# Two graph-attention layers on one core: mask steps placed earlier in the interleaving, softmax sums of two head groups in one PSUM bank, value differences per batch

## Chip, cores and metric

The kernel runs on one core of one Trainium2 chip. The metric is the device time of an execution in microseconds; lower is better. The runs of the kernel before have a median of 2573.73 us (2572.56 to 2574.11, three runs).

## What is computed

64 graphs (the batch) of 256 nodes with 512 features each pass through two attention layers over one adjacency matrix; all data is fp32. In both, the input is normalised over its features and cut at zero, and the layer's output is added to the input:

```
h = max(layernorm(x), 0)
x = x + concat(softmax(mask(leaky_relu(s_i + n_j))) @ (h W), h W)      # layer 0, one head of 256
h = max(layernorm(x), 0)
q, k, v = h Wq' + bq, h Wk' + bk, h Wv' + bv                           # layer 1, 8 heads of 64
x = x + softmax(mask(q k' / 8)) @ v @ Wo' + bo
```

## The kernel before

**Tiling and stages.** The 64 graphs are handled in 32 groups of two ("batches" b = 0 and 1 of group g). A group passes through five stages, and in the steady part four groups are under way at once:

- `first_norm` (layer 0's normalisation of group g+3): statistics on DVE, the factors (a power and a product on POOL), the scaled and cut rows `xn` on ACT, a transposition by DVE and by a pass through DRAM (`passed`, `moved`, issued by SP), and the copy into `hT0` on ACT.
- `first_layer` (group g+2): products `ph`, copied to `H` by ACT, a broadcast transposition `pn` of a column of `H` for the neighbour scores, exponentials `e`, products `po`, and layer 1's normalisation, which ends in `hT1`. Its last piece, the 14th, calls `operand_sums(gpsimd, ...)`: four POOL operations of 128x512 that make `sums` and change a quarter of `hT1` (lines 473 to 479, 613 to 614). There is one `sums` buffer (line 596).
- `project` (group g+1): q, k and v by a scheme with seven block products instead of eight (lines 634 to 708); its third, fifth and seventh products read `sums`, and the very last, for v, ends the project stage of a group. ACT keeps partial results in tiles with the tag `kept`; DVE adds them.
- `scores` (group g, batch b): eight score tiles `sc` on PE and their exponentials into `p` on ACT, then four mask pieces (`mask_pairs`, line 738): DVE multiplies a pair of heads by the 0/1 mask, POOL adds the second key half to the first, in place.
- `weigh` (line 752) and `outputs` (line 785) of the batch whose scores came last: the sums of the exponentials over the keys (`total`, a product with ones), their reciprocal `r` on DVE, the weighted values `pr`, their scaling into `oT`, and the output products `py`, which DVE adds onto `x`.

With P0 and P1 the two key halves of the exponentials, `p` holds P0 + P1 in the place of P0 after the mask pieces. So `total` needs one product instead of two, and `v` must hold V0 and V1 - V0: (P0 + P1) V0 + P1 (V1 - V0) is the wanted sum. `value_differences` (line 710) makes V1 - V0 in place on POOL, for both batches of a group. In `pr` the four heads of a quad ("quad" is half of the eight heads) lie in the four column strips of PE; the products with V0 come first, then those with V1 - V0.

**What sets the order.** A scheduler orders each engine's instructions. The kernel ties it down: PE's instructions are chained one behind another as they are written (`in_order`, line 131), and `not_sooner` (line 123) puts an instruction behind the last one that was *written* for the same engine, which each engine's wrapper `Remembers` keeps in `last` (line 27). Instructions without such a tie may be moved by the scheduler. Engines then execute in that order.

What is written when is given by two strings, one for each batch of a group (line 882). A letter calls the next piece of one stage: `S` scores, `m` a mask piece, `n` first_norm, `s` first_layer, `u` project, `o` outputs. At half of each string (position 16 or 18, line 908) come the residual's bias additions for group g+1 (`residual`, four POOL operations), then the value differences of group g, both only in the first string, and the load of a later group. `weigh` comes ahead of each string, for the batch before. In the second string the 14th `s` stands at position 25 and an `n` that makes factors at position 23; in the first string the factors are made by the `n` at position 21.

**Buffers.** `q`, `k` and `v` of a group and batch lie in "places", single buffers of 4 KB per partition, taken from a list and given back when their reader is written (lines 625 to 629, 735, 779). PSUM has five banks in turn (`mm`, line 109) and three held ones. `r` has one buffer (line 764).

Of the kernel before, what the change touches and what calls it, by code (L numbers as in the profile page):

```python
# [8 lines left out]
F32 = mybir.dt.float32  # L9
# [5 lines left out]
P = 128  # L15
# [42 lines left out]
def bounded(  # L58
# [107 lines left out]

    w0_sb = const.tile([P, HP, F1 + 2], F32, name="w0_sb")
    nc.sync.dma_start(w0_sb[:, :, 2:], w0.rearrange("(c p) o -> p c o", p=P))
    adj_i = att.tile([P, NT, N], I32, tag="kept", name="adj_i")
    nc.sync.dma_start(adj_i, adj.rearrange("(t p) k -> p t k", p=P))  # L170

    def score_columns():
# [6 lines left out]
                )  # L179

    def mask():
        edge = att.tile([P, NT, N], F32, tag="kept", name="edge")
        not_sooner(vector, "tensor_scalar", edge, adj_i, 0.0, None, op0=ALU.not_equal)
        yield
        pt = mm("pt_mask").rearrange("p (k q) -> p k q", k=NT)
        for kb in range(NT):
            for t in range(NT):
                transpose(
                    pt[:, kb, t * P : (t + 1) * P], edge[:, t, kb * P : (kb + 1) * P], ident
                )  # L190
        not_sooner(vector, "tensor_copy", maskT, pt)

        not_sooner(vector, "reduce_max", bad[:, 0, :], edge, axis=AX.X)
        vector.tensor_scalar(bad[:, 0, :], bad[:, 0, :], 0.0, None, op0=ALU.is_equal)
        vector.tensor_tensor(edge, edge, adj_i, op=ALU.not_equal)
        vector.reduce_max(bad[:, 1, :], edge, axis=AX.X)
        yield
# [63 lines left out]
    def last_bias():  # L261


        wide = att.tile([P, 2, 2, P], F32, tag="kept", name="bv_wide")
        for q in range(NQ):
            for half in range(2):
                gpsimd.tensor_scalar(
                    wide[:, half, q, :], square_ones, bv_col[:, half, q : q + 1], None, op0=ALU.mult
                )
        yield  # L270
        pb = mm("pb")
        for q in range(NQ):
            for half in range(2):
                matmul(
                    pb, wide[:, half, q, :], w_sb["o"][:, half, 2 * q : 2 * q + 2, :],
                    start=(q == 0 and half == 0), stop=(q == NQ - 1 and half == 1),
                )
        yield
        not_sooner(vector, "tensor_add", b_out, pb, b_out)
        yield  # L280
# [341 lines left out]
                not_sooner(gpsimd, "tensor_add", xt, xt, b_out)  # L622


    places = [f"place{i}" for i in range(8)]

    def place(shape, name):
        tag = places.pop(0)
# [5 lines left out]
    def project(g):  # L634
        ops = operands.pop(g)
        for name in ("q", "k", "v"):
            shape = [P, NT, D] if name == "v" else [P, HP, N]
            dst = {}
            for b in range(GB):
                dst[b], tag = place(shape, f"{name}_{g}_{b}")  # L640
                qkv[name, g, b] = dst[b], tag
            turn[0] = 1 - turn[0]

            def blocks(bank):
                return bank.rearrange("p (o n) -> p o n", o=2)

            def product(out, i, start):
                a, w = ops[i][0], w_sb[name][:, :, ops[i][1], :]
                for o in range(2):
                    cols = slice(o * P, (o + 1) * P)  # L650
                    for c in range(2):
                        of, by = (a[:, c, cols], w[:, c, :]) if name == "v" else (w[:, c, cols], a[:, c, :])
                        matmul(
                            out[:, o, :], of, by, start=start and o == c == 0, stop=o == c == 1,
                            skip_group_check=True,
                        )

            def part(b, half):
                if name == "v":
                    return dst[b][:, :, half * D // 2 : (half + 1) * D // 2]  # L660
                return dst[b][:, 2 * half : 2 * half + 2, :]

            def take(to, bank, half):

                behind = [scalar.last] if g <= 1 else []
                if name == "v":
                    taken = [scalar.copy(to, bank)]
                else:
                    taken = [
                        scalar.activation(  # L670
                            to[:, o, :], bank[:, o, :], AF.Identity,
                            bias=bcol[name][:, 2 * half + o : 2 * half + o + 1], scale=1.0,
                        )
                        for o in range(2)
                    ]
                for last in behind:
                    for instruction in taken:
                        after(instruction, last)

            def kept(bank, half, i):  # L680
                s = att.tile([P, 2, N], F32, tag="kept", name=f"kept{i}_{name}_{g}")
                take(s, bank, half)
                return s

            first = blocks(held_bank(turn[0], f"p{name}1_{g}"))
            product(first, 1, True)
            p1 = kept(first, 0, 0)
            yield
            second = blocks(mm(f"p{name}2_{g}"))
            product(second, 2, True)  # L690
            vector.tensor_add(part(0, 0), second, p1)
            yield
            product(first, 6, False)
            p16 = kept(first, 0, 1)
            yield
            second = blocks(held_bank(1 - turn[0], f"p{name}7_{g}"))
            product(second, 7, True)
            p7 = kept(second, 1, 2)
            yield
            product(first, 5, False)  # L700
            vector.tensor_add(part(1, 1), first, p7)
            yield
            product(second, 4, False)
            vector.tensor_add(part(1, 0), second, p16)
            yield
            product(first, 3, False)
            take(part(0, 1), first, 1)
            yield

    def value_differences(g):  # L710

        for b in range(GB):
            v = qkv["v", g, b][0]
            not_sooner(gpsimd, "tensor_sub", v[:, 1, :], v[:, 1, :], v[:, 0, :])

    def scores(g, b):

# [34 lines left out]
    def weigh(g, b, p):  # L752


        v, v_tag = qkv["v", g, b]
        for quad in range(NQ):
            name = f"{g}_{b}_{quad}"
            total = mm(f"total_{name}")[:, :N]
            for j in range(QH):
                matmul(  # L760
                    total[j * S : (j + 1) * S, :], ones, p[:, quad * QH + j, 0, :],
                    start=True, stop=True,
                )
            r = att.tile([P, N], F32, tag="r", name=f"r_{name}", bufs=1)
            vector.reciprocal(r, total)
            pr = mm(f"pr_{name}").rearrange("p (h n) -> p h n", h=2)
            for half in range(2):
                for kb in range(NT):
                    for j in range(QH):
                        head = quad * QH + j  # L770
                        c0 = head * DH + half * S
                        matmul(
                            pr[j * S : (j + 1) * S, half, :], v[:, kb, c0 : c0 + S],
                            p[:, head, kb, :], start=(kb == 0), stop=(kb == NT - 1),
                        )
            oT = big.tile([P, 2, N], F32, tag=f"oT{quad}", name=f"oT_{name}", bufs=1)
            vector.tensor_mul(oT, pr, r[:, None, :].to_broadcast([P, 2, N]))
            oTs[quad] = oT
        places.append(v_tag)
        quads = [oTs[c][:, :, r * P : (r + 1) * P] for r in range(2) for c in range(2)]  # L780
        sums = big.tile([P, 3, 2, P], F32, tag="o_sums", name=f"o_sums_{g}_{b}", bufs=1)
        operand_sums(vector, quads, sums)
        operands["o", g, b] = seven(quads, sums)
# [95 lines left out]
    run(verdict)  # L879


    steps = ("Smmnuuuuonuouuomssnumnosunosnouso", "Smmsususuososuomssusumonusonuouunous")
    waiting, late = None, iter(())
    for g in range(NG):
        products = project(g + 1) if g + 1 < NG else iter(())
        pieces = first_layer(g + 2) if g + 2 < NG else iter(())
        for b, parts in enumerate(steps):
            if g == b == 0:

                parts = "Smmnn" + parts[4:].replace("uon", "unon", 1)  # L890
            if waiting is not None:
                weigh(*waiting)
                late = outputs(*waiting[:2])
            for i, part in enumerate(parts):
# [10 lines left out]
                else:  # L905
                    waiting = (g, b, scores(g, b))
                    masks = mask_pairs(waiting[2])
                if i == len(parts) // 2:
                    if b == 0:
                        if g + 1 < NG:  # L910
                            residual(g + 1)
                        value_differences(g)
                    if g + 3 < NG:
                        load(g + 3, b)
        run(products)
# [374 lines left out]
```

## Time and profile before

| | |
|---|---|
| median of three runs | 2573.73 us |
| the profiled execution's own time | 2571.85 us |
| its span, first to last instruction | 2570.2 us |
| mean granted TensorE clock | 0.998 |
| instructions | 41394 |
| value differences on POOL, 128x512 | 64, mean 1267 ns |
| reciprocals on DVE, 128x256 | 128, mean 1756 ns |
| mask multiplications on DVE, 128x1024 | 256, mean 1209 ns |
| mask sums on POOL, 128x512 | 256, mean 1603 ns |
| operand sums on POOL, 128x512 | 4 x 32, mean 1283 to 1289 ns |

The span and the waits are those of one profiled execution; its own time is 1.88 us below the median of the runs. PE's matmuls overlap: one of 256 columns is recorded with about 380 ns, and eight in a row begin 1.73 us apart from the next eight. PEld is the loading of weights. A matmul of fp32 leaves two records. In the steady part the timeline repeats itself once per group, so one group between two `sc` blocks can stand for nearly all.

### The profile page before, as it was taken

Reading aid. Unit: us, or ns where it says so; the run is one execution under the profiler, and the core shown is the slowest. Engines: PE = TensorE matmul, PEld = TensorE weight load, DVE = VectorE, ACT = ScalarE, POOL = GpSimd, SP = SyncE. Lnnn points to the kernel's source line nnn. Section 1 sums busy time; section 2 is a strip of 40 time slices with the busy share of each in tenths; the row PEclk is TensorE's granted clock in tenths of the full one; section 3 lists DMA queues with packets and bytes.
Section 4 is the critical chain, followed back from the end, with each engine's and each line's share of the span. In section 5 each row is a group of like instructions: output and inputs, shape, how many; then the busy total and the mean of one; then the engine's idle time right before and its main releaser. Section 6 shows DMA issues by size and latency. Waiting matters only on the chain.

```text
span 2570.2 us, 41394 instructions
## 1 busy us (share of the span) xinstructions
PE 2490.8 (97%) x16158; PEld 2052.6 (80%) x16158; DVE 1691.7 (66%) x2971; ACT 1012.5 (39%) x2019; POOL 1008.7 (39%) x978
## 2 busy tenths in 40 slices
PE   8999999999999999999999999999999999999998
PEld 7777878878778778788787887887887878878886
DVE  6566666776666666667766666666677666766656
ACT  5433443443433434434434344344344343443421
POOL 3524444243443334442444433344424444333432
PEclk9999999999999999999999999999999999999999
DMA  5122222322232321223222223212232222232110
GB/s 184 66 83 72 66 85 74 99 81 75 68 99 75 99 72 62 89 74 99 75 80 68 91 83 99 72 60 91 74 99 73 80 71 91 83 99 69 41 41 34
DMA packets 129353, 205.40 MB, mean 80 GB/s; under 512 B 13952, under 2 KB 78208, under 8 KB 129152
## 3 DMA queue, kind: packets, MB, share of 16 engines
q1 hardware_dynamic: 129152, 202.69, 24.7%
q8 instruction: 129, 2.11, 0.3%
q14 instruction: 72, 0.59, 0.1%
HBM read 104.08 MB, written 98.57 MB: 79 GB/s over the span
## 4 chain that ended last, share of the span: by engine, by line
PE 77%; POOL 14%; DVE 3%; issue 3%; ACT 2%; DMA 1%; POOLq 0%; SPq 0%; DVEq 0%; ACTq 0%
PE pq L137 15%; PE pv L137 15%; PE py L137 12%; PE sc L137 10%; PE pk L137 9%; PE pr L137 8%; POOL x L35 6%; PE po L137 4%; POOL p L35 4%; POOL v L35 3%; PE total L137 2%; DVE p L35 2%; ACT xn L35 1%; POOL factor L35 1%; PE ph L137 1%
## 5 line engine op out<-in xcount | busy, mean ns | idle before, releaser
L35 POOL TENSOR_TENSOR p<-p 128x512 f32<-128x512 f32 x256 | 407.8, 1603 | 970.9 <-DVE p L35 881.0
L35 ACT ACTIVATE p<-sc 128x512 f32<-128x512 f32 x512 | 264.0, 612 | 211.2 <-PE sc L137 203.3
L35 ACT ACTIVATE xn<-x,factor 128x512 f32<-128x512 f32 x256 | 194.4, 806 | 387.1 <-POOL factor L35 387.1
L35 DVE TENSOR_TENSOR x<-py,x 128x256 f32<-128x256 f32 x448 | 186.4, 416 | 243.8 <-PE py L137 234.6
L35 DVE TENSOR_TENSOR p<-p,maskT 128x1024 f32<-128x1024 f32 x256 | 301.5, 1209 | 0.0
L137 PE MATMUL sc<-q,k 64*128 64x256 f32 x2048 | 266.5, 390 | 8.0 <-ACT p L35 8.0
L35 DVE RECIPROCAL r<-total 128x256 f32<-128x256 f32 x128 | 224.8, 1756 | 66.3 <-PE total L137 59.9
L137 PE MATMUL py<-wo_sb,oT 128*128 128x256 f32 x1024 | 262.8, 379 | 3.5 <-DVE x L35 3.1
L137 PEld LDWEIGHTS sc<-q,k 64*128 64x128 f32 x2048 | 213.0, 186 | 62.1 <-issue 25.9
L35 DVE STREAM_TRANSPOSE xt<-xn 128x512 f32<-128x512 f32 x248 | 164.4, 692 | 134.2 <-ACT xn L35 134.2
L137 PE MATMUL pr<-p,v 128*32 128x256 f32 x4096 | 245.5, 379 | 0.4 <-POOL v L35 0.4
L137 PE MATMUL pk<-hT,wk_sb 128*128 128x256 f32 x1024 | 244.9, 382 | 0.0
L137 PE MATMUL pv<-wv_sb,hT 128*128 128x256 f32 x1024 | 238.6, 381 | 4.9 <-ACT kept_v L35 4.9
L137 PE MATMUL pq<-hT,wq_sb 128*128 128x256 f32 x1024 | 239.9, 382 | 0.0
L137 PE MATMUL ph<-w_sb,hT 128*128 128x258 f32 x1024 | 239.4, 381 | 0.3 <-ACT hT L35 0.3
L137 PEld LDWEIGHTS pv<-wv_sb,hT 128*128 128x128 f32 x1024 | 195.3, 191 | 32.2 <-ACT kept_v L35 5.3
L137 PEld LDWEIGHTS pk<-hT,wk_sb 128*128 128x128 f32 x1024 | 191.7, 190 | 36.1 <-issue 10.7
L137 PEld LDWEIGHTS pq<-hT,wq_sb 128*128 128x128 f32 x1024 | 191.8, 190 | 35.0 <-issue 9.9
L137 PEld LDWEIGHTS py<-wo_sb,oT 128*128 128x128 f32 x1024 | 193.8, 190 | 32.3 <-DVE x L35 3.9
L137 PEld LDWEIGHTS ph<-w_sb,hT 128*128 128x128 f32 x1024 | 194.4, 190 | 29.6 <-ACT hT L35 0.9
L137 PEld LDWEIGHTS pr<-p,v 128*32 128x32 f32 x4096 | 133.3, 110 | 88.6 <-POOL v L35 0.9
L35 POOL TENSOR_TENSOR factor<-factor,rexp 128x2 f32<-128x2 f32 x128 | 91.7, 716 | 281.2 <-DVE factor L35 281.2
(122 smaller groups left out, 3747.6 us busy)
## 6 DMA issues: line engine op xcount, KB each, us to landing
passed<-xt SPq DMA_DIRECT2D x124, 512.0 KB, 3.0
moved<-passed SPq DMA_DIRECT2D x496, 128.0 KB, 3.2
x<-in_x_dram SPq DMA_DIRECT2D x64, 512.0 KB, 4.3
out_dram<-x SPq DMA_DIRECT2D x64, 512.0 KB, 3.1
wq_sb<-in_L_gnn_Wq_dram SPq DMA_DIRECT2D x2, 512.0 KB, 9.2
wk_sb<-in_L_gnn_Wk_dram SPq DMA_DIRECT2D x2, 512.0 KB, 10.7
wv_sb<-in_L_gnn_Wv_dram SPq DMA_DIRECT2D x2, 512.0 KB, 7.5
wo_sb<-in_L_gnn_Wo_dram SPq DMA_DIRECT2D x8, 128.0 KB, 3.9
```

The costliest lines, as they stand in the source:

```text
L35: instruction = getattr(self.engine, operation)(*args, **kwargs)
L137: in_order(nc.tensor.matmul(*args, **kwargs))
```

## The change

Four things change:

- The third and fourth mask pieces of each batch are written earlier: in the first string at positions 8 and 11 instead of 15 and 20, in the second at 13 and 16 instead of 15 and 21. The other letters keep their order among themselves.
- `weigh` makes `total` of both quads in the two halves of one bank, then both reciprocals (now tied with `not_sooner`) in one tile `r`, then `pr` and `oT` of each quad.
- The value differences are made for one batch at a time, in each string at three quarters of its length (position 24 or 27) instead of both at half of the first.
- There are seven places instead of eight, each taken only when its part is first written, and three `kept` buffers instead of two.

```diff
-    places = [f"place{i}" for i in range(8)]
+    places = [f"place{i}" for i in range(7)]
...
-            dst = {}
-            for b in range(GB):
-                dst[b], tag = place(shape, f"{name}_{g}_{b}")
-                qkv[name, g, b] = dst[b], tag
...
             def part(b, half):
+                if (name, g, b) not in qkv:
+                    qkv[name, g, b] = place(shape, f"{name}_{g}_{b}")
+                to = qkv[name, g, b][0]
...
-                s = att.tile([P, 2, N], F32, tag="kept", name=f"kept{i}_{name}_{g}")
+                s = att.tile([P, 2, N], F32, tag="kept", name=f"kept{i}_{name}_{g}", bufs=3)
...
-    def value_differences(g):
-
-        for b in range(GB):
-            v = qkv["v", g, b][0]
-            not_sooner(gpsimd, "tensor_sub", v[:, 1, :], v[:, 1, :], v[:, 0, :])
+    def value_differences(g, b):
+
+        v = qkv["v", g, b][0]
+        not_sooner(gpsimd, "tensor_sub", v[:, 1, :], v[:, 1, :], v[:, 0, :])
...
+        name = f"{g}_{b}"
+        total = mm(f"total_{name}").rearrange("p (q n) -> p q n", q=NQ)
+        r = att.tile([P, NQ, N], F32, tag="r", name=f"r_{name}", bufs=1)
         for quad in range(NQ):
-            name = f"{g}_{b}_{quad}"
-            total = mm(f"total_{name}")[:, :N]
             for j in range(QH):
                 matmul(
-                    total[j * S : (j + 1) * S, :], ones, p[:, quad * QH + j, 0, :],
+                    total[j * S : (j + 1) * S, quad, :], ones, p[:, quad * QH + j, 0, :],
                     start=True, stop=True,
                 )
-            r = att.tile([P, N], F32, tag="r", name=f"r_{name}", bufs=1)
-            vector.reciprocal(r, total)
-            pr = mm(f"pr_{name}").rearrange("p (h n) -> p h n", h=2)
+        for quad in range(NQ):
+            not_sooner(vector, "reciprocal", r[:, quad, :], total[:, quad, :])
+        for quad in range(NQ):
+            pr = mm(f"pr_{name}_{quad}").rearrange("p (h n) -> p h n", h=2)
...
-            vector.tensor_mul(oT, pr, r[:, None, :].to_broadcast([P, 2, N]))
+            vector.tensor_mul(oT, pr, r[:, quad, None, :].to_broadcast([P, 2, N]))
...
-    steps = ("Smmnuuuuonuouuomssnumnosunosnouso", "Smmsususuososuomssusumonusonuouunous")
+    steps = ("Smmnuuuumonmuouuossnunosunosnouso", "Smmsususuososmuomssusuonusonuouunous")
...
-                parts = "Smmnn" + parts[4:].replace("uon", "unon", 1)
+                parts = "Smmnn" + parts[4:].replace("uumon", "uumnon", 1)
...
+                if i == len(parts) * 3 // 4:
+                    value_differences(g, b)
                 if i == len(parts) // 2:
-                    if b == 0:
-                        if g + 1 < NG:
-                            residual(g + 1)
-                        value_differences(g)
+                    if b == 0 and g + 1 < NG:
+                        residual(g + 1)
                     if g + 3 < NG:
                         load(g + 3, b)
```

More of the change, by code (lines that the diff above doesn't have):

```diff
@@ L168, in bounded @@
     nc.sync.dma_start(w0_sb[:, :, 2:], w0.rearrange("(c p) o -> p c o", p=P))
-    adj_i = att.tile([P, NT, N], I32, tag="kept", name="adj_i")
+    adj_i = att.tile([P, NT, N], I32, tag="kept", name="adj_i", bufs=3)
     nc.sync.dma_start(adj_i, adj.rearrange("(t p) k -> p t k", p=P))
@@ L181, in mask @@
     def mask():
-        edge = att.tile([P, NT, N], F32, tag="kept", name="edge")
+        edge = att.tile([P, NT, N], F32, tag="kept", name="edge", bufs=3)
         not_sooner(vector, "tensor_scalar", edge, adj_i, 0.0, None, op0=ALU.not_equal)
@@ L261, in last_bias @@
     def last_bias():
-        wide = att.tile([P, 2, 2, P], F32, tag="kept", name="bv_wide")
+        wide = att.tile([P, 2, 2, P], F32, tag="kept", name="bv_wide", bufs=3)
         for q in range(NQ):
@@ L658, in part @@
             def part(b, half):
+                if (name, g, b) not in qkv:
+                    qkv[name, g, b] = place(shape, f"{name}_{g}_{b}")
+                to = qkv[name, g, b][0]
                 if name == "v":
-                    return dst[b][:, :, half * D // 2 : (half + 1) * D // 2]
-                return dst[b][:, 2 * half : 2 * half + 2, :]
+                    return to[:, :, half * D // 2 : (half + 1) * D // 2]
+                return to[:, 2 * half : 2 * half + 2, :]
             def take(to, bank, half):
@@ L775, in weigh @@
                         )
-            oT = big.tile([P, 2, N], F32, tag=f"oT{quad}", name=f"oT_{name}", bufs=1)
-            vector.tensor_mul(oT, pr, r[:, None, :].to_broadcast([P, 2, N]))
+            oT = big.tile([P, 2, N], F32, tag=f"oT{quad}", name=f"oT_{name}_{quad}", bufs=1)
+            vector.tensor_mul(oT, pr, r[:, quad, None, :].to_broadcast([P, 2, N]))
             oTs[quad] = oT
```

## The prediction

> **What bounds the kernel now.** I read the busy table, the waits of the whole span, the chain of work in order of time (which shows the period), and one period of the timeline engine by engine. The first row of the page, then one period in the table by stretches (columns: length, busy PE, PEld, DVE, ACT, POOL with counts, granted clock, DMA share, GB/s):
>
> ```profile
> PE 2490.8 (97%) x16158; PEld 2052.6 (80%) x16158; DVE 1691.7 (66%) x2971; ACT 1012.5 (39%) x2019; POOL 1008.7 (39%) x978
> ```
>
> ```profile
> 1000.00:1078.64 78.64, 76.94 (x501) 63.49 (x500) 52.38 (x92) 31.31 (x63) 31.24 (x31) 1.00 0.26 81
> ```
>
> The chain repeats itself every 78.64 us (a block of 32 score matmuls stands at 1042.83 and at 1121.47), once per group. PE is busy for 76.94 of it. Nothing but 1.70 us per group can be won by waiting less, and anything that makes PE wait is paid in full. The waits say whose they are (total us, times, longest):
>
> ```profile
> POOL sums L35 <- ACT hT L35: 216.6, 30, 9.3
> ...
> PE pn L140 <- ACT H L35: 41.2, 29, 1.5
> ...
> POOL sums L35 <- PE pv L137: 13.1, 1, 13.1
> ...
> PE sc L137 <- ACT p L35: 8.0, 31, 0.3
> ```
>
> So PE waits 1.4 us per group for the last column of `pn` and 0.26 us in the scores. The timeline shows the chain behind `pn` (start, length, engine; in brackets the idle time before):
>
> ```profile
> 1065.97 4.95 POOL L35 TENSOR_TENSOR x<-x,b_out 128x512 f32<-128x512 f32 x4
> 1070.88 2.50 POOL L35 TENSOR_TENSOR v<-v 128x512 f32<-128x512 f32 x2
> ...
> 1075.23 0.71 POOL L35 TENSOR_TENSOR factor<-factor,rexp 128x2 f32<-128x2 f32 x1
> ...
> 1076.25 1.52 ACT L35 ACTIVATE xn<-x,factor 128x512 f32<-128x512 f32 x2 [6.46 <-POOL factor L35]
> 1077.67 0.35 ACT L35 COPY H<-ph 128x258 f32<-128x258 f32 x1
> ...
> 1078.07 0.32 PE L140 MATMUL pn<-ident,H 128*128 128x128 f32 x1 [1.45 <-ACT H L35]
> ```
>
> POOL does the residual, both value differences and a mask sum ahead of the factor; ACT stands in front of `xn` for 6.46 us with the copy of `H` behind it; PE wants that copy. At the other end of the group:
>
> ```profile
> 1110.47 0.71 POOL L35 TENSOR_TENSOR factor<-factor,rexp 128x2 f32<-128x2 f32 x1 [1.00 <-DVE factor L35]
> ...
> 1118.76 1.29 POOL L35 TENSOR_TENSOR sums<-hT 128x512 f32<-128x512 f32 x1 [7.30 <-ACT hT L35]
> 1120.12 1.28 POOL L35 TENSOR_TENSOR sums<-sums,hT 128x512 f32<-128x512 f32 x1
> 1121.36 1.27 POOL L35 TENSOR_TENSOR hT<-hT 128x512 f32<-128x512 f32 x1
> 1122.58 1.28 POOL L35 TENSOR_TENSOR sums<-hT,sums 128x512 f32<-128x512 f32 x1
> ...
> 1117.54 1.14 ACT L35 COPY hT<-moved 128x512 f32<-128x512 f32 x2
> ...
> 1116.95 0.64 PE L137 MATMUL total<-p,ones 128*32 128x256 f32 x8
> 1117.41 1.91 PE L137 MATMUL pr<-p,v 128*32 128x256 f32 x32
> ```
>
> The reader is to see that POOL idles for 7.30 us in front of the four operand sums, and that these run until 1123.86, while PE reads `v` from 1117.41 on. They cannot be much earlier: there is one `sums` buffer, and the last `pv` product, which reads it, ends as `total` begins. Where everything else was ready (the one wait "POOL sums <- PE pv", group 0) they began at 173.48, right behind the last `pv` product.
>
> **What the Trainium skill says.** "TensorE: Matmul & The Clock Gate", section "Architectural detail: the array is 16× 32×32, not 1× 128×128", says that GpSimd's queue is strictly first in, first out; the trace agrees (the POOL factor of 1075.23, whose input was written by 1067.26, stood behind the residual and the differences). The same page, "What's actually happening", says that an idle window of some 3.4 us halves the clock and a busy one restores it. The trace has two such places:
>
> ```profile
> 85.65 3.46 PE L137 MATMUL pv<-wv_sb,sums 128*128 128x256 f32 x8 [2.69 <-ACT kept_v L35]
> ...
> 167.06 3.68 PE L137 MATMUL pv<-wv_sb,hT 128*128 128x256 f32 x8 [4.92 <-ACT kept_v L35]
> ```
>
> After idle times of 2.69 and 4.92 us, eight matmuls took 3.3 to 3.5 us where they take 1.73 elsewhere, with the clock at 0.50; idle times of 1.45 us left it at 1.00. "GPSIMD Engine Reference", section 3.1, has some 2.6 cycles per element for a two-input operation; the trace has 1267 ns for a value difference, and that is used.
>
> **The change, part by part.**
>
> *Masks 3 and 4 earlier.* The order of the `u`, `o` and `s` letters, and with it PE's order outside `weigh`, stays as it was. In step 0 the two DVE masks (1.2 us each) leave 1061.93 for about 1051 to 1056, where DVE was idle for 3.56 us; the two POOL sums follow directly (1.26 to 2.1 us each) and are done ahead of the residual. In step 1 they move up some 2 to 4 us, before the norm's transposes. On PE this costs nothing: `total` needs the sums only at 1079.19 and 1116.95. No DMA moves with them.
>
> *Value differences of batch 0.* They go from position 16 to 24, behind the factor. In front of the factor POOL now has neither differences nor the fourth mask sum (2.50 + 1.26 us), and the residual starts earlier: factor near 1068, `xn` right behind the third copy of `H` (1069.8), the fourth copy when `ph` is there (about 1073.8), `pn` at 1076.6 without a wait. Gain 41.2 us, all 29 waits. Next late would be `pn`'s own place behind 1076.13, which is PE work. The difference itself (1.27 us, near 1071) is due at 1079: free.
>
> *Value differences of batch 1: the step that decides.* `not_sooner` queues an instruction behind the last one that was *written* for its engine. At position 27 of step 1 this isn't the factor (position 23, run at 1110.47): the 14th `s`, at position 25, has written `operand_sums(gpsimd, …)`. So the difference of batch 1 stands behind the four sums, which wait for the last `pv` product and the copy of `hT`. It starts at 1123.8 and ends at 1125.07 (+1.27); PE gets it at about 1125.15. The first to read it is the fifth `pr` product (the four before it read the other half of `v`): `total` for both quads from 1116.95 takes 2 x 0.46 = 0.92, four products (8 records at 54 ns) 0.43, so it is due at 1118.3. PE stalls 6.9 us, and everything on it queues behind. In groups 1 to 29 that is 29 x 6.9 = 200.1; in group 0, where the sums start at 173.48, the difference ends at about 179.85 against 174.6: 5.25. Groups 30 and 31 have no operand sums any more. Together **+205.3 us**. Nothing hides it: PE's order is written out.
>
> *The clock after it.* An idle time of 6.9 us is longer than both that halved the clock. There the half clock took 3.0 to 3.4 us of work, half of it lost: 1.5 to 1.7 us. A window that ends within the stall would cost less, one that is mostly idle a second window: 0.8 to 2.2. I take 1.6: 30 x 1.6 = **+48 us**.
>
> *Both sums in one bank, both reciprocals ahead.* The same 1024 matmuls, 128 reciprocals (1756 ns) and products. The first reciprocal waits 0.46 us longer (for both quads); the second no longer waits for the first `oT`. The four banks of a `weigh` become three; `pr`'s first bank comes free one reciprocal later (1.76 us), so the scores of step 1 may wait more than their 0.26 us, or less, having one more free bank: between -8 us in all and +1 us per group (+30). At step 0 the stall gives DVE the time. I take 0.
>
> *Three kept buffers, seven places.* A place is taken at its first write; the seventh is that of the values just weighed, and the product that writes into it comes later in PE's order than their last reader. 0.
>
> Sum, against the profiled execution's own 2571.85 us (span 2570.2): 2571.85 + 205.3 + 48 - 41.2 = 2784. The median of the runs is 1.9 above the profiled one: **2786**.
>
> **The rivals.**
> (a) *Shorter hold.* ACT copies the last `hT` ahead of the values of 1117.06, and the sums start as in group 0, 0.2 us after the last `pv` product: stall 5.25 us in all 30 groups, 157.5, and 1.4 of clock, 42: 2571.85 + 157.5 + 42 - 41.2 + 1.9 = 2732. For it: the data of the last fetch landed about 1115.3 (issued until 1112.1, 3.2 us to land); against: ACT's order there is fixed, and nothing ahead of it moves much.
> (b) *Banks as well*: 1 us per group in the scores on top, 2816.
> (c) *Faster.* The difference of batch 1 leaves POOL ahead of the sums: POOL is idle from 1111.5 to 1118.76, so it would end by 1112.7. It decides at 1118.3: done before that, PE loses nothing, and only the gain is left: 2573.7 - 41.2 = 2532 (2524 with the scores' wait gone too). For it: the idle time; against: the written order, by which the sums come first.
>
> **How the numbers follow.** Forecast 0.68, (a) 0.14, (b) 0.08, (c) 0.08, else 0.02. The forecast's own spread is the clock, 0.8 to 2.2 us per group (2762 to 2804). The range goes from (a) with a cheap clock, 2732 - 17 = 2715, to (b) with a little more, 2825; it leaves (c) out. 0.2% is about what a measurement of this kernel can tell from no change. Slower 0.91, same 0.01, faster 0.08.
>
> **What would show it.** A new row "PE pr <- POOL v" in the waits, near 30 times and 200 us, longest about 7; "PE pn <- ACT H" gone; POOL's timeline with `v<-v` x1 right behind `sums<-hT,sums`; a period of 85.7 us; a clock below 1.00 in every group. The prediction is wrong if `v<-v` runs ahead of the sums, or if the clock stays at 1.00 behind the stalls.

## The result and the profile after

The changed kernel takes 2785.27 us (median of four runs, 2781.51 to 2786.45); beside it the kernel before took 2573.14 us (four runs, 2571.79 to 2574.11). The ratio is 1.0822, with a 95% interval of 1.0804 to 1.0841. The profiled execution took 2781.51 us, with a span of 2779.9 us and a mean granted clock of 0.96. The forecast was 2786.

First the busy row of the page, then one period from the table by stretches (columns: length, busy PE, PEld, DVE, ACT, POOL with counts, clock, DMA share, GB/s):

```profile
PE 2525.4 (91%) x16158; PEld 2060.1 (74%) x16158; DVE 1656.0 (60%) x2971; ACT 1012.8 (36%) x2019; POOL 989.4 (36%) x978
```

```profile
1044.04:1129.37 85.33, 77.84 (x501) 63.63 (x501) 51.00 (x92) 31.32 (x63) 30.54 (x31) 0.96 0.23 74
```

The work is the same (16158 matmul records, 978 POOL instructions), but a group takes 85.33 us instead of 78.64. PE's busy time rose by only 0.90 us per group; the rest of the 6.69 us is idle. The waits (total us, times, longest) say where:

```profile
POOL sums L35 <- ACT hT L35: 235.2, 30, 11.6
...
PE pr L137 <- POOL v L35: 197.3, 30, 6.6
...
PE sc L137 <- DVE r L35: 25.4, 30, 0.9
```

The row "PE pr <- POOL v" is new. The row "PE pn <- ACT H" is gone, and the scores wait longer, now for a reciprocal. POOL's timeline at the end of the second string shows what PE waits for:

```profile
1105.85 0.71 POOL L35 TENSOR_TENSOR factor<-factor,rexp 128x2 f32<-128x2 f32 x1 [2.79 <-DVE factor L35]
...
1114.69 1.27 POOL L35 TENSOR_TENSOR sums<-hT 128x512 f32<-128x512 f32 x1 [7.86 <-ACT hT L35]
1116.03 1.26 POOL L35 TENSOR_TENSOR sums<-sums,hT 128x512 f32<-128x512 f32 x1
1117.25 1.27 POOL L35 TENSOR_TENSOR hT<-hT 128x512 f32<-128x512 f32 x1
1118.48 1.26 POOL L35 TENSOR_TENSOR sums<-hT,sums 128x512 f32<-128x512 f32 x1
1119.70 1.26 POOL L35 TENSOR_TENSOR v<-v 128x512 f32<-128x512 f32 x1
```

And PE's, in the same stretch:

```profile
1112.88 1.07 PE L137 MATMUL total<-p,ones 128*32 128x256 f32 x16
1113.77 0.61 PE L137 MATMUL pr<-p,v 128*32 128x256 f32 x8
1121.01 4.51 PE L137 MATMUL pr<-p,v 128*32 128x256 f32 x56 [6.63 <-POOL v L35]
1125.45 3.92 PE L137 MATMUL sc<-q,k 64*128 64x256 f32 x32
```

POOL idles for 7.86 us with the value difference standing behind the four sums, makes the sums, and then the difference, until 1120.96. PE has made four products (eight records at 54 ns, 0.43 us from 1113.77) and is due to go on at 1114.20; it does so at 1121.01. The stall is 6.81 us (the page says 6.63, since it counts from the modelled end of the records). The 56 records behind it begin over 1125.45 - 1121.01 = 4.44 us; at 54 ns each they would take 3.02. The granted clock shows why:

```profile
1113.42:1116.83 3.41, 0.96 (x20) 0.31 (x12) 2.81 (x2) 2.61 (x5) 2.06 (x2) 1.00 0.66 186
1116.83:1121.01 4.18, 0.00 (x0) 0.00 (x0) 1.72 (x3) 0.00 (x0) 4.13 (x4) 0.50 0.39 128
1121.01:1123.65 2.64, 2.64 (x28) 1.24 (x32) 0.00 (x0) 0.00 (x0) 0.00 (x0) 0.50 0.94 273
1123.65:1125.45 1.80, 1.80 (x37) 0.83 (x29) 0.69 (x1) 0.00 (x0) 0.00 (x0) 1.00 0.95 247
```

It falls to 0.50 within the stall, at 1116.83, and is 1.00 again from 1123.65. Of these 6.82 us of half clock 4.18 pass while PE stands still; only the other 2.64 fall on work. At the other end of the group, the chain that held `pn` before:

```profile
1147.07 0.71 POOL L35 TENSOR_TENSOR factor<-factor,rexp 128x2 f32<-128x2 f32 x1
...
1153.24 1.27 POOL L35 TENSOR_TENSOR v<-v 128x512 f32<-128x512 f32 x1
...
1152.37 1.52 ACT L35 ACTIVATE xn<-x,factor 128x512 f32<-128x512 f32 x2
1156.43 0.37 ACT L35 COPY H<-ph 128x258 f32<-128x258 f32 x1 [2.54 <-PE ph L137]
...
1158.82 0.60 PE L140 MATMUL pn<-ident,H 128*128 128x128 f32 x4
```

The factor comes 11.8 us ahead of `pn` (2.8 us before), ACT is done with `xn` before the last `ph` exists, and `pn` runs as one row of four without a bracket: nobody waits.

### The profile page after: what moved, and what is told of

The parts are those of the page before. It is cut to its first block, busy times and chain, and to the rows that moved or that the text cites. A ratio compares the mean times of both kernels' runs of the same rounds, so it can differ in the third digit from the quotient of the medians.

```text
span 2779.9 us, 41263 instructions
## 1 busy us (share of the span) xinstructions
PE 2525.4 (91%) x16158; PEld 2060.1 (74%) x16158; DVE 1656.0 (60%) x2971; ACT 1012.8 (36%) x2019; POOL 989.4 (36%) x978
## 4 chain that ended last, share of the span: by engine, by line
PE 81%; DVE 8%; POOL 7%; ACT 2%; issue 2%; DMA 0%; SPq 0%; ACTq 0%; DVEq 0%; POOLq 0%
PE pq L137 14%; PE pk L137 14%; PE py L137 14%; PE pv L137 14%; PE ph L137 8%; PE sc L137 8%; PE pr L137 5%; POOL sums L35 4%; PE po L137 4%; DVE r L35 4%; DVE e L35 2%; POOL v L35 1%; POOL hT L35 1%; ACT hT L35 1%; DVE x L35 1%
## 5 line engine op out<-in xcount | busy, mean ns | idle before, releaser
L35 POOL TENSOR_TENSOR p<-p 128x512 f32<-128x512 f32 x256 | 383.6, 1509 | 928.1 <-DVE p L35 926.3
L137 PE MATMUL pr<-p,v 128*32 128x256 f32 x4096 | 282.5, 431 | 197.3 <-POOL v L35 197.3
L137 PEld LDWEIGHTS pr<-p,v 128*32 128x32 f32 x4096 | 142.4, 124 | 325.3 <-POOL v L35 211.8
L35 DVE TENSOR_TENSOR p<-p,maskT 128x1024 f32<-128x1024 f32 x256 | 340.5, 1351 | 0.0
L137 PE MATMUL sc<-q,k 64*128 64x256 f32 x2048 | 256.2, 389 | 26.6 <-DVE r L35 25.4
L137 PEld LDWEIGHTS pk<-hT,wk_sb 128*128 128x128 f32 x1024 | 191.7, 190 | 36.1 <-issue 10.8
L137 PE MATMUL py<-wo_sb,o_sums 128*128 128x256 f32 x768 | 198.3, 381 | 3.6 <-DVE x L35 3.6
```

Of the source, the lines that this page charges most:

```text
L35: instruction = getattr(self.engine, operation)(*args, **kwargs)
L137: in_order(nc.tensor.matmul(*args, **kwargs))
```

## The experiments

All times are medians; ratios stand against runs of the kernel before on the same chip. Those have medians of 2572.79 to 2573.36 us, so that the rows can be set side by side. "Period" is the distance of two `sc` blocks of the second string in the steady part.

| kernel | us | ratio to before (95%) | period |
|---|---|---|---|
| before | 2573 | 1 | 78.64 |
| after | 2785.27 | 1.0822 (1.0804 to 1.0841) | 85.33 |
| e1_sooner | 2534.20 | 0.9849 (0.9836 to 0.9861) | 77.22 |
| e2_diff_alone | 2801.76 | 1.0889 (1.0873 to 1.0905) | 85.57 to 87.14 |
| e3_fill | 2742.03 | 1.0657 (1.0642 to 1.0673) | 84.13 |
| e4_old_weigh | 2527.08 | 0.9822 (0.9810 to 0.9835) | 77.01 |
| e5_two_sums | 2724.49 | 1.0590 (1.0573 to 1.0606) | 84.18 and 83.06 |
| e6_weigh_alone | 2581.23 | 1.0039 (1.0025 to 1.0052) | 78.81 |
| e7_masks_alone | 2526.34 | 0.9819 (0.9805 to 0.9832) | 77.01 |
| e8_diff_sooner | 2527.20 | 0.9822 (0.9809 to 0.9836) | 77.01 |
| e9_late_edge | 2523.79 | 0.9809 (0.9795 to 0.9822) | 76.92 |
| e10_swap | 2511.33 | 0.9759 (0.9746 to 0.9773) | 76.49 |
| e11_swap_late | 2504.32 | 0.9736 (0.9722 to 0.9749) | 76.24 |

### The hold

**e1_sooner**: the whole change, with the differences written at two thirds of each string (positions 22 and 24 instead of 24 and 27), which puts that of batch 1 ahead of the 14th `s`. If the order of writing is the cause, this alone must turn the loss into a gain.

```diff
-                if i == len(parts) * 3 // 4:
+                if i == len(parts) * 2 // 3:
                     value_differences(g, b)
```

> The changed kernel, with the value differences written at two thirds of each string (positions 22 and 24) instead of three quarters (24 and 27): in the second string ahead of the 14th first_layer piece, and so ahead of the operand sums on POOL. Theory (the difference of batch 1 stands behind the operand sums): PE's wait for v goes, the clock stays at 1.00, what is left is the gain of pn, 41 us, less some 0.24 us per group in the scores of the second string: about 2573 - 41 + 7 = 2539 us. Rival (the sums of both quads in one bank and the earlier reciprocals cost the time): the time stays near 2785 us, since weigh is untouched. Rival (masks, places): the same, near 2785 us.

Measured: 2534.20 us, 5 below the expectation and 251 below the rival's. POOL's timeline of this kernel:

```profile
1016.82 0.71 POOL L35 TENSOR_TENSOR factor<-factor,rexp 128x2 f32<-128x2 f32 x1 [2.79 <-DVE factor L35]
...
1017.75 1.28 POOL L35 TENSOR_TENSOR v<-v 128x512 f32<-128x512 f32 x1
...
1025.61 1.28 POOL L35 TENSOR_TENSOR sums<-hT 128x512 f32<-128x512 f32 x1 [6.58 <-ACT hT L35]
```

The same instruction, written three letters earlier in the string, runs in POOL's idle time, done 6.6 us before the sums begin. PE has no wait for `v` any more. So the hold and what hangs on it cost 2785.27 - 2534.20 = 251.1 us, and the other parts of the change together gain 38.8.

**e2_diff_alone**: the kernel before, with only the differences as the change has them. If they alone make the loss, the other parts are not needed for it.

```diff
...
+                if i == len(parts) * 3 // 4:
+                    value_differences(g, b)
...
-                        value_differences(g)
```

> The kernel before with one part of the change alone: value differences for one batch at a time at three quarters of each string; masks, weigh, places and kept buffers as before. Theory: the whole loss, and the gain of pn as well, since the differences left the factor's way: total of one quad only ahead of the wait, so PE stalls about 7.3 us in 29 groups and 5.7 in one (217 us), clock 1.4 us in 30 groups (42), pn -41: about 2573 + 217 + 42 - 41 = 2791 us. Rival (weigh or masks are the cost): near 2573 us.

Measured: 2801.76 us, 10.8 us over the expectation. The waits and PE's timeline:

```profile
PE pr L137 <- POOL v L35: 212.1, 32, 7.1
```

```profile
1122.41 0.61 PE L137 MATMUL pr<-p,v 128*32 128x256 f32 x8
1130.09 2.79 PE L137 MATMUL pr<-p,v 128*32 128x256 f32 x24 [7.06 <-POOL v L35]
```

The stall is 1130.09 - 1122.84 = 7.25 us, as expected: 0.44 longer than in the changed kernel, because here only one quad's `total` stands ahead of the four products. What was off most is the clock: the periods repeat as 87.14, 86.25, 85.80 and 85.57, with a mean of 86.19. Less the 77.01 of e8_diff_sooner, which is the same kernel without the stall, and less the 7.25 of the stall, 1.93 us per group are left for the clock.

### The clock behind the stall

**e3_fill**: the changed kernel, in which PE makes the first four `pr` products of batch 1 fifteen times over in groups 1 to 29. The values stay the same. If the half clock comes from the idle time, PE is to be faster with 56 more products per group.

```diff
+                    held = b == 1 and 0 < g < NG - 2 and quad == half == kb == 0
+                    again = 14 if held else 0
+                    for i in range(again + 1):
...
-                            p[:, head, kb, :], start=(kb == 0), stop=(kb == NT - 1),
+                                p[:, head, kb, :], start=(kb == 0), stop=(kb == NT - 1 or i < again),
```

> The changed kernel with more work: in groups 1 to 29, in weigh of batch 1, the first four pr products are made 15 times instead of once (each time from the start, so that the values are the same), 14 x 0.43 = 6.0 us of products in the time in which PE would wait for v. It tells the stall from the clock behind it. Theory (the stall halves the clock, which costs 1.4 us behind it): the stall is filled up to 0.8 us, the clock stays at 1.00, and the kernel gets faster by 29 x 1.4 = 41 us, to about 2744 us. Rival (the products behind the wait are slow for another reason, POOL or DVE traffic say): about 2785 us as the changed kernel.

Measured: 2742.03 us, 43.2 less than the changed kernel, at a mean clock of 0.997. PE's timeline, and then the table by stretches for the steady 2500 us of the changed kernel and of this one:

```profile
1101.95 6.66 PE L137 MATMUL pr<-p,v 128*32 128x256 f32 x120
1109.27 3.23 PE L137 MATMUL pr<-p,v 128*32 128x256 f32 x56 [0.66 <-POOL v L35]
```

```profile
200.00:2700.00 2500.00, 2282.77 (x14671) 1863.69 (x14671) 1482.75 (x2641) 909.14 (x1803) 891.46 (x872) 0.96 0.23 73
```

```profile
200.00:2700.00 2500.00, 2454.01 (x18163) 1988.03 (x18161) 1505.38 (x2670) 919.38 (x1822) 904.45 (x879) 1.00 0.22 73
```

PE resumes when the difference is there, as before, but the 56 records take 3.16 us to the next row instead of 4.44, and the clock of the stretch goes from 0.96 to 1.00. The period of 84.13 is that of e1_sooner, 77.22, and the 6.9 us of the hold, with nothing over. This parts the 251.1 us: 207.8 for the hold (2742.03 - 2534.20), 43.2 for the clock. Group 0 has no filler and keeps its clock loss: its half clock ends 4.84 us after PE resumes at 181.40, half of which, 2.4 us, belongs to the clock and not to the hold. The Trainium skill's "TensorE: Matmul & The Clock Gate", in "What's actually happening", puts it as "the default state is throttled, and activity releases the throttle"; the trace agrees, since useless activity was enough.

**e5_two_sums**: the changed kernel, with the difference of batch 1 between the second and the third operand sum, so that the stall is two sums shorter. It asks whether a shorter stall loses less clock.

```diff
...
-        engine.tensor_sub(sums[:, 1], sums[:, 0], a11)
+        not_sooner(engine, "tensor_sub", sums[:, 1], sums[:, 0], a11)
+        if engine is gpsimd and between:
+            value_differences(*between.pop())
...
+                if b == 1 and i == 24 and g + 2 < NG:
+                    between.append((g, b))
...
```

> The changed kernel with the value difference of batch 1 between the second and the third of the four operand sums instead of behind the fourth (the third and fourth have no part in it). Theory for the stall: it ends 2.45 us sooner, 4.36 us in 29 groups, and the period without any clock loss is 85.33 - 1.41 - 2.45 = 81.47 us. For the clock there are two ideas. The one on record (some 1.4 us lost behind each stall): period 82.9, 2573 + 30 x 4.24 = 2700 us. The one from the trace after the change, where the period settles on 85.33 us, 25 windows of 3.413 us: a stall takes back what it was late, half per group, so that the period settles on the next whole number of windows, 24 x 3.413 = 81.92, with a loss of 0.45 us: 2573 + 30 x 3.28 = 2671 us. Rival (the hold has nothing to do with the sums): 2785 us.

Measured: 2724.49 us; both numbers missed. POOL's and PE's timelines:

```profile
1094.89 1.26 POOL L35 TENSOR_TENSOR sums<-sums,hT 128x512 f32<-128x512 f32 x1
1096.11 1.27 POOL L35 TENSOR_TENSOR v<-v 128x512 f32<-128x512 f32 x1
1097.34 1.26 POOL L35 TENSOR_TENSOR hT<-hT 128x512 f32<-128x512 f32 x1
```

```profile
1092.63 0.61 PE L137 MATMUL pr<-p,v 128*32 128x256 f32 x8
1097.43 5.80 PE L137 MATMUL pr<-p,v 128*32 128x256 f32 x56 [4.19 <-POOL v L35]
```

The order and the stall are as expected (1097.43 - 1093.06 = 4.37 us, 2.44 shorter than 6.81). But the 56 records are longer than behind the long stall: rows of 5.80 and 4.68 us alternate, where the changed kernel settles at 4.51. The mean period of 83.62, less 77.22 and 4.37, leaves 2.03 us per group for the clock; the same sum for the changed kernel gives 85.33 - 77.22 - 6.81 = 1.30. So the loss isn't a fixed charge per stall, nor does it shrink with the stall. The clock behind two stalls in a row shows what it follows:

```profile
1097.43:1102.70 5.27, 5.27 (x52) 2.51 (x56) 0.69 (x1) 0.00 (x0) 2.40 (x2) 0.50 0.83 259
...
1181.62:1184.62 3.00, 3.00 (x30) 1.39 (x34) 0.14 (x1) 0.00 (x0) 2.40 (x2) 0.50 0.88 229
```

The shorter stall ends sooner, so more of the half clock is still to come when PE resumes: 5.27 and 3.00 us in turn, 2.64 in the changed kernel. Work at half clock takes about twice as long (52 records in 5.27 us are 101 ns each, against 54), so half of these times is lost: 2.07 us on the average (2.03 by the periods) and 1.32 (1.30). In e2_diff_alone the same sum gives 1.96 (1.93), from 5.85, 4.05, 3.13 and 2.68 us.

### The other parts alone

**e7_masks_alone**: the kernel before with the new strings only.

```diff
-    steps = ("Smmnuuuuonuouuomssnumnosunosnouso", "Smmsususuososuomssusumonusonuouunous")
+    steps = ("Smmnuuuumonmuouuossnunosunosnouso", "Smmsususuososmuomssusuonusonuouunous")
```

> The kernel before with the earlier masks alone; both value differences stay at half of the first string, behind the residual. Theory: the fourth mask sum leaves the way of the factor and the residual starts earlier, so the factor comes before the fourth ph product ends and the wait of pn goes as a whole: 2573 - 41 = 2532 us. Rival (the differences, 2.5 us of POOL in front of the factor, are what held pn): the gain is the 1.26 us of one mask sum at most, 29 x 1.26 = 37, or less than half of that.

Measured: 2526.34 us. The gain is 47.0 us, 5.8 more than the waits table had put down to `pn`, and the wait of `pn` is gone. POOL's timeline:

```profile
1039.81 4.94 POOL L35 TENSOR_TENSOR x<-x,b_out 128x512 f32<-128x512 f32 x4
1044.72 2.49 POOL L35 TENSOR_TENSOR v<-v 128x512 f32<-128x512 f32 x2
...
1047.77 0.70 POOL L35 TENSOR_TENSOR factor<-factor,rexp 128x2 f32<-128x2 f32 x1
```

Both differences still stand ahead of the factor, and yet the factor runs 10.6 us ahead of `pn` (1058.34): with the third and fourth mask sums out of the way, the residual starts early enough.

**e8_diff_sooner**: the kernel before, with the differences per batch at two thirds and nothing else.

```diff
...
+                if i == len(parts) * 2 // 3:
+                    value_differences(g, b)
...
-                        value_differences(g)
```

> The kernel before with the value differences for one batch at a time as in e2_diff_alone, but at two thirds of each string (behind the factor in both strings, ahead of the operand sums). Theory: the loss of e2_diff_alone (229 us) is all from the place behind the sums, and the differences out of the factor's way are enough for pn: 2573 - 42 = 2531 us, no wait of PE for v. Rival (one batch at a time costs something by itself, a difference too late for its weigh): above 2540 us with PE waiting for v.

Measured: 2527.20 us. Taking the differences from in front of the factor brings the same as moving the masks (2526.34), and both together bring no more (2527.08, e4_old_weigh below). `pn` stood 1.63 us per group late (78.64 to 77.01), and either move takes away more than that.

**e6_weigh_alone**: the kernel before, with the new `weigh` and the seven places whose room it needs.

```diff
...
-            total = mm(f"total_{name}")[:, :N]
+        total = mm(f"total_{name}").rearrange("p (q n) -> p q n", q=NQ)
+        r = att.tile([P, NQ, N], F32, tag="r", name=f"r_{name}", bufs=1)
...
-            vector.reciprocal(r, total)
+        for quad in range(NQ):
+            not_sooner(vector, "reciprocal", r[:, quad, :], total[:, quad, :])
...
```

> The kernel before with the new weigh (and the seven places that it needs room for) alone; masks and value differences as before. Theory: weigh costs only what the scores of the second string wait longer, 7 us as between e1_sooner and e4_old_weigh: about 2580 us. Rival (a reciprocal that doesn't wait for the first oT is a gain on DVE): below 2571 us.

Measured: 2581.23 us (five runs, 2581.00 to 2585.84), slower by 7.9. The waits:

```profile
PE pn L140 <- ACT H L35: 41.5, 29, 1.5
...
PE sc L137 <- DVE r L35: 23.1, 30, 0.9
```

`pn` waits as before, and the scores wait for the reciprocal: with three banks where there were four, the third score tile gets the bank of `total`, which comes free with the second reciprocal.

**e4_old_weigh**: e1_sooner with the `weigh` of before, which is the diff of `weigh` above turned round.

> As e1_sooner, and weigh as it was before (each quad's sum in a bank of its own, its reciprocal ahead of its own products): masks, places and differences are changed, weigh is not. Theory: about 2573 - 41 = 2532 us, 7 us below e1_sooner, because the scores of the second string wait 0.3 us for an exponential and no longer 0.86 us for the second reciprocal. Rival (weigh is the cost): some 2530 us here and near 2785 in e1_sooner.

Measured: 2527.08 us, 7.1 below e1_sooner; the difference between the two is as expected, both lie 5 us lower. So the new `weigh` costs 7 to 8 us in both surroundings. The three kernels that take the wait of `pn` away and keep the old `weigh` all lie within 1 us of each other (2526.34 to 2527.20), so places, kept buffers and a difference per batch cost nothing that these runs can tell. DVE's timeline here, at the first string's end, shows why the scores wait even with the old one:

```profile
1060.18 1.38 DVE L35 SCALAR_TENSOR_TENSOR e<-e 128x512 f32<-128x512 f32 x2
1061.47 1.75 DVE L35 RECIPROCAL r<-total 128x256 f32<-128x256 f32 x1
1063.14 1.22 DVE L35 TENSOR_TENSOR e<-e,maskT 128x512 f32<-128x512 f32 x2
...
1065.07 1.76 DVE L35 RECIPROCAL r<-total 128x256 f32<-128x256 f32 x1
```

`total` was there from about 1060.2; the first reciprocal stands behind two operations on layer 0's exponentials (from the last `s` of the string), and two mask multiplications stand behind it, ahead of `oT` and the second reciprocal.

### A version that is faster than both

**e9_late_edge**: e4_old_weigh with these mask multiplications written behind `weigh`, and one `s` of the second string two letters earlier.

```diff
             scalar.activation(e, e, AF.Exp)
-            vector.tensor_mul(e, e, maskT)
             pT[b] = e
         yield
+        for b in range(GB):
+            not_sooner(vector, "tensor_mul", pT[b], pT[b], maskT)
...
-"Smmsususuososmuomssusuonusonuouunous"
+"Ssmmususuososmuomssusuonusonuouunous"
```

> As e4_old_weigh, and layer 0's two mask multiplications (1.2 us together), which stand on DVE between the first reciprocal and the first oT of the second string's weigh, are written behind weigh's own DVE work, with one s letter ahead of the first two mask pieces. Theory (the scores of the second string are paced by the banks that the reciprocals and oT hold: 4.60 us for 32 records that take 3.85 in the first string): 31 x 0.75 = 23 us less than e4_old_weigh at most, about 2505 us, and no row of PE's scores waiting. Rival (they are paced by ACT's exponentials): as e4_old_weigh, 2527 us.

Measured: 2523.79 us, only 3.3 less: the miss of this group. The second reciprocal did come 0.9 us earlier, counted from `total` (4.40 us behind its start at 1059.55, against 5.34 in e4_old_weigh), but the first one is where it was, behind the operations on `e`:

```profile
1060.00 1.38 DVE L35 SCALAR_TENSOR_TENSOR e<-e 128x512 f32<-128x512 f32 x2
1061.30 1.75 DVE L35 RECIPROCAL r<-total 128x256 f32<-128x256 f32 x1
...
1063.95 1.76 DVE L35 RECIPROCAL r<-total 128x256 f32<-128x256 f32 x1
```

**e10_swap**: e7_masks_alone with the last `s` and `u` of the first string exchanged, so that the operations on `e` run while PE makes the products of that `u`.

```diff
-"Smmnuuuumonmuouuossnunosunosnouso"
+"Smmnuuuumonmuouuossnunosunosnosuo"
```

> As e7_masks_alone, with the last s and u of the first string in the other order, so that pn and layer 0's exponentials come ahead of a projection product and of ACT's copy of it. Theory (the scores of the second string take 4.60 us instead of 3.85 because the first reciprocal starts 0.8 us late behind layer 0's DVE work, which waits on ACT behind that copy): the reciprocal starts right behind its sum, the scores take 3.85 to 4.0, and the time falls by up to 30 x 0.75 = 22 us to 2504; pn may wait 0.1 us for H. Rival (the scores are paced by ACT): 2526 us as e7_masks_alone.

Measured: 2511.33 us, 15.0 less than e7_masks_alone, between the two expectations. No wait of the scores is left in the table, but the block of 32 takes 4.18 us there and 3.92 elsewhere.

**e11_swap_late**: e9_late_edge with the same exchange.

> As e9_late_edge (old weigh, changed masks and places, differences ahead of the sums, layer 0's mask multiplications behind weigh), with the same two letters exchanged as in e10_swap. Theory: nothing of layer 0 on DVE between the sums and the scaling any more, all waits of the scores gone: 2523.8 - 30 x 0.68 = 2503 us. Rival: 2524 us as e9_late_edge.

Measured: 2504.32 us, ratio 0.9736: 2.6% below the kernel before, and 1.3 us off the expectation. DVE's timeline, then PE's:

```profile
1049.84 1.42 DVE L35 SCALAR_TENSOR_TENSOR e<-e 128x512 f32<-128x512 f32 x2 [0.88 <-ACT e L35]
...
1052.16 1.76 DVE L35 RECIPROCAL r<-total 128x256 f32<-128x256 f32 x1 [0.17 <-PE total L137]
```

```profile
1051.46 0.64 PE L137 MATMUL total<-p,ones 128*32 128x256 f32 x8
...
1055.91 3.92 PE L137 MATMUL sc<-q,k 64*128 64x256 f32 x32
```

The first reciprocal now follows `total` at once, and the scores go through without a gap. It took both edits: the exchange without the late masks leaves 0.26 us per group in the scores (4.18 against 3.92), the late masks without the exchange leave 0.68 of 0.78 (4.60, where e4_old_weigh has 4.70).

## Why the prediction was right, and where it was off

Three differences between kernels that ran stand for the terms of its sum, and add up to the whole:

| step of the prediction | predicted | measured |
|---|---|---|
| hold of batch 1's difference | +205.3 | +207.8 (e3_fill less e1_sooner) |
| the clock after it | +48 | +43.2 (after less e3_fill) |
| `pn`'s wait gone, `weigh` at nothing | -41.2 + 0 | -38.8 (e1_sooner less before) |
| sum | +212 | +212 |

With the 2.4 us of group 0 put where they belong, the hold measures 205.4 and the clock 45.6. That the forecast came out within 1 us is luck in part: the clock was put 2.4 us too high, and `pn` and `weigh` together gain 2.4 us less than was put.

- **The decisive step** was right in its mechanism and its size. `not_sooner` queued the difference behind the sums of the 14th `s`; predicted 6.9 us of stall, measured 6.81 in the steady part; for group 0 predicted 5.25, measured 5.24 (due at 175.18, resumed at 180.42). e1_sooner shows that the place in the text is the cause, e2_diff_alone that no other part is needed. The first rival, a shorter hold in every group, fell: ACT copied its last `hT` at 1113.47, behind the values of 1112.99, in the same order as before (1117.54 and 1117.06). The second, a full microsecond per group in the scores, fell too: 7 us are 0.23 per group. The rival on the other side, the difference ahead of the sums, is what e1_sooner is; its 2534.20 stands beside the 2532 that was worked out for it.
- **The clock** was right as a mechanism (e3_fill), a little large: 45.6 / 30 = 1.52 us per group on the average instead of 1.6. But the way it was priced, one window of half clock that falls nearly whole on work, isn't what happens: in the steady part there are two, they begin within the stall, and 4.18 of their 6.82 us cost nothing. The loss depends on where they end: 1.30 us here, 1.93 in e2_diff_alone, 2.03 in e5_two_sums, all within the 0.8 to 2.2 that were allowed. That 1.6 came close here is partly luck.
- **`pn`**: its wait went wholly, by the chain that was laid out. The size was low: 41.2 is the waits table's figure, while e7_masks_alone gained 47.0 and the period fell by 1.63 us per group, not 1.4.
- **`weigh` at nothing** was the term that was mis-sized: e1_sooner less e4_old_weigh gives +7.1, e6_weigh_alone +7.9. The bank that comes free later costs more than the earlier reciprocals bring. It lies within the stated -8 to +30 and hides behind the low figure for `pn`: e4_old_weigh less before is -45.9, and -45.9 + 7.1 is the -38.8.
- **"Nothing but 1.70 us per group can be won by waiting less"** was wrong. e11_swap_late has the same products and a period of 76.24, 2.40 below 78.64. PE's busy time is made of modelled, overlapping records and hides short gaps. The table by stretches of e10_swap and of e11_swap_late shows it:

```profile
200.00:2450.00 2250.00, 2250.00 (x14721) 1871.80 (x14720) 1562.92 (x2645) 909.00 (x1810) 915.74 (x872) 1.00 0.25 81
```

```profile
200.00:2450.00 2250.00, 2250.00 (x14758) 1872.77 (x14759) 1535.55 (x2646) 907.19 (x1810) 917.92 (x871) 1.00 0.25 81
```

PE is busy for the whole of both, and yet the second has 37 matmul records more in it and is 7 us shorter in all.

## What to carry to other kernels

An instruction tied behind "the last one of its engine" waits for whatever was written just ahead of it, so look up which instruction that is and what *it* waits for; here standing behind one letter of a string instead of ahead of it cost 251 us. Where one wait is removed by two edits, each may bring all of it, so the gains of parts are measured alone before they are added. Short gaps are read from the starts of matmul blocks and from the period, not from the busy share, which was full in a kernel that still had 0.25 us per group to lose.

## What the runs showed of the hardware that was not expected

- **The half clock comes in windows that run on their own.** Every half-clock stretch of the changed kernel but the last, which its end cuts short, lasts one, two or three times 3.413 us, and each starts a whole number of such times after the first: 2656.24 less 86.00, say, is 753 times 3.4133. They don't begin with the stall or with the work.
- **Stalls that come back lock the period to these windows.** From one end of a stall to the next, the changed kernel starts with 86.29, 85.82, 85.57 and 85.46 us, settles at 85.33, which is 25 windows, and after one disturbed group goes through 87.02, 86.19, 85.76 and 85.56 back to it. The distance from 85.33 halves each time (0.96, 0.49, 0.24, 0.13). That is what the sum behind e5_two_sums would give: a stall that ends later leaves less half clock, so half of the delay is made up. In e5_two_sums two periods make 84.18 + 83.06 = 167.24, 49 windows; in e2_diff_alone four make 344.76, 101 of them.
- **A shorter stall can lose more clock**: 2.03 us behind 4.37, 1.30 behind 6.81. What decides fits the time that PE stood still within a window (the stalls and the windows of the changed kernel, e2_diff_alone and e5_two_sums, laid over each other). A window at full clock with up to 1.61 us of stall in it was followed by full clock, one with 2.08 us or more by half clock. A window at half clock with up to 0.78 us was followed by full clock, one with 0.79 us or more by half clock again. The steady state of the changed kernel has 0.77 to 0.78 us there (1120.24 to 1121.01, say); its one disturbed group, with 0.78 (1973.57 to 1974.35), stayed at half clock for a window more. So it stands right at the limit. No run here set the stall against the windows on purpose, so these limits are read from three traces and not tested.
- **More work was faster**: with 3248 more matmul records in the trace of e3_fill than in that of the changed kernel (19406 and 16158: 56 products of two records in 29 groups), the kernel ran 43.2 us shorter. The stall itself stayed; e1_sooner, which removes it, is another 207.8 us faster.
